# Second expert layer: TensorE's instructions in written order, the small work in pieces between a tile's control products

## The chip, the cores and the metric

The kernel runs on one core of one Trainium2 chip. The metric is the device time of the whole program in microseconds, as a median over runs: 3760.18 us of three runs, 3752.28 to 3766.32. Five engines work side by side and meet through semaphores: TensorE (PE, matrix products, with its weight loads as PEld), VectorE (DVE), ScalarE (ACT), GpSimd (POOL) and SyncE (SP, which issues transfers).

## The reference

The program is a network of four levels, each made of an attention over a context, a self-attention and a feed-forward layer. `x` is 16 x 64 x 256, so 1024 tokens of 256 numbers. The change is in the feed-forward layer of level 1, "the second expert layer" here:

```python
x = x + _L1_ffn_ref(_layernorm(x, axis=-1), ...)

def _inl(ctrl, xs, vs, mu):
    a, b, g = jnp.split(ctrl, 3, axis=-1)
    v_next = jax.nn.sigmoid(a) * vs - jax.nn.softplus(b) * (xs - mu)
    x_next = xs + DT * jax.nn.sigmoid(g) * v_next          # DT = 0.1
    return (x_next, v_next)

logits = _gelu(xf @ router_w1 + router_b1) @ router_w2 + router_b2
topk_p, topk_i = jax.lax.top_k(jax.nn.softmax(logits, axis=-1), K)   # K = 2 of E = 8
topk_p = topk_p / jnp.sum(topk_p, axis=-1, keepdims=True)
v = jnp.zeros_like(xf); integrated = xf
for _ in range(ITERS):                                      # ITERS = 2
    ctx = jnp.concatenate([integrated, v], axis=-1)
    shared_ctrl = _gelu(ctx @ shared_w1 + shared_b1) @ shared_w2 + shared_b2
    x_sh, v_sh = _inl(shared_ctrl, integrated, v, mu)
    ...
    ctrl = _experts(ctx_e, flat_idx, expert_w1, expert_b1, expert_w2, expert_b2)
    x_r, v_r = _inl(ctrl, x_e, v_e, mu)                     # both picks, weighted with topk_p
    x_next = sw * x_sh + (1.0 - sw) * x_r                   # v_next in the same way
    halt = jax.nn.sigmoid(_gelu(integrated @ halt_w1 + halt_b1) @ halt_w2 + halt_b2)
    integrated = integrated + halt * (x_next - integrated)
    v = v + halt * (v_next - v)
refined = _gelu(integrated @ refine_w1 + refine_b1) @ refine_w2 + refine_b2
out = xf + integration_weight * refined
```

Every token thus takes two rounds. In each it gets three controls of 3 x 256 numbers: one shared, and one from each of the two experts the router picked for it. Each expert's inner row has 64 numbers.

## The kernel before

`l1_ffn` (L1460) holds the layer. The 1024 tokens are two halves, `a` and `b`, of four tiles of 128 tokens each (`Half`, L1532). A half keeps on the chip its state `xi` and `v` and the sum `dx` (tokens on the partitions), and `cT`, the same `xi` and `v` turned, so that the 512 numbers of `ctx` lie on the partitions.

The steps of the layer are functions, called one after the other:

- `start(s)` normalises the half's four tiles into `xi`, turns them into `cT` (`self.transpose`, L152: four 128 x 128 transposes for two tiles at L160, then one copy out of PSUM on VectorE, L124, and one on ScalarE, L126) and has GpSimd add `xi` to the residual.
- `route(s)` makes the router: a product with Gelu (`gelu_t`: the product at L1549, the Gelu at L1550), the logits `pl` (L1570), softmax, ranks, a one-hot `hots` of each pick (L1578), turned into `hotT` (L1584, copied at L1586), and the two weights `wk`.
- `hidden(s, it)` makes the inner rows: `sT` of the shared expert and halt gate, four chunks `eT` of all eight experts (each chunk a product of 128 x 512 and its Gelu; two passes in round 0, four in round 1, in which `v` is no longer zero), then the halt product `ph` (L1606) and its sigmoid.
- `pick(s, i)` multiplies `eT` by the pick's one-hot: four products that spread the one-hot over the inner rows (L1614), each followed by a product on VectorE that writes `eh` (L1615).
- `control(s, it, i)` makes a control: `i` is -1 for the shared one, 0 and 1 for the picks. For each pair of tiles it fills one buffer `pc` of three banks. Each block of 256 columns starts with a product of the biases (L1632), followed by one product of the shared inner rows (L1636) or by four of `eh` (L1639). Round 0 has two blocks, round 1 three. Then ScalarE takes tanh of the gates (L1643, L1645) and the absolute value (L1646), and VectorE the positive part `rb` (L1647). After both pairs: exponent (L1649) and logarithm (L1650) on ScalarE, `vn` on GpSimd (L1651), and on VectorE `sp` (L1652), `vn` (L1653), in round 1 two more rows with `a`, `g` (L1658), and the sums into `dx` and `v` (L1661 for the shared control, L1664 for a pick, one row of 128 x 256 for each tile).
- `update(s, it)` moves `xi` by `dx` and the halt gate (L1671), turns it, and in round 0 does the same with `v` (L1676).
- `refine(s)` makes the output: four Gelu chunks `fT`, four output tiles `po` (L1686), each with three rows after it: `y` on VectorE, `y` on GpSimd, and the sum into the residual.

PSUM holds two buffers under the tag "mm", which the products of `gelu_t`, the turns, `pl`, `hotT`, `pick`, `ph` and `po` share in the order in which they are written, and two under "pc" for the controls. A product that starts a new buffer waits for the readers of the one before last.

The biases of the controls, `bias2`, are built ahead of the halves, in three steps of `part`, `raw` and `bias2` on VectorE (L1505 to L1507), and `expand`, the matrix of the picks, at L1514.

The order of the calls is this, from L1692 on:

```python
start(a); hidden(a, 0); route(a); start(b)
control(a, 0, -1); pick(a, 0); route(b); pick(a, 1); control(a, 0, 0); hidden(b, 0); control(a, 0, 1)
pick(b, 0); control(b, 0, -1); update(a, 0); pick(b, 1); control(b, 0, 0); hidden(a, 1); pick(a, 0)
control(b, 0, 1); control(a, 1, -1); pick(a, 1); update(b, 0); control(a, 1, 0); hidden(b, 1); pick(b, 0)
control(a, 1, 1); control(b, 1, -1); pick(b, 1); update(a, 1); control(b, 1, 0); control(b, 1, 1)
refine(a); update(b, 1); refine(b)
```

It is the order in which the instructions are recorded. A scheduler then orders each engine's instructions by its own plan, and may bring an instruction forward past others of its engine. An instruction handed to `keep_in_program_order` keeps its place among the others that were handed to it. The helpers `self.mm` and `self.tr` (L2450) do that for products and transposes while `self.pinned` is true; other stages use them, and this layer calls `nc.tensor.matmul` and `nc.tensor.transpose` itself, which leaves TensorE's order to the scheduler.

Of the kernel before, what the change touches and what calls it, by code (L numbers as in the profile page):

```python
# [64 lines left out]
class Sections:  # L65
# [1394 lines left out]
    def l1_ffn(self):  # L1460
# [3 lines left out]
        with ExitStack() as ctx:  # L1464
# [79 lines left out]
            def gelu_t(out, w, cT, bias, nk, lo=0):  # L1544

                m = out.shape[0]
                pm = ps.tile([m, N], F32, tag="mm", name="gelu_t")
                for c in range(nk):
                    nc.tensor.matmul(pm, w[:, c, lo : lo + m], cT[:, c, :], start=(c == 0), stop=(c == nk - 1))  # L1549
                nc.scalar.activation(out, pm, AF.Gelu, bias=bias)  # L1550

            def start(s):
                mv = sb2.tile([P, TT, 2], F32, tag="ln_mv", name="ln_mv")
                for t in range(TT):
                    st = sb2.tile([P, 6], F32, tag="ln_st", name="ln_st", bufs=3)
                    nc.vector.bn_stats(st, s.x[:, t, :])
                    nc.vector.bn_aggr(mv[:, t, :], st)
                r = self.rstd(sb2, mv[:, :, 1], 1e-5, "ln_r")
                for t in range(TT):
                    nc.vector.tensor_scalar(  # L1560
                        s.xi[:, t, :], s.x[:, t, :], mv[:, t, 0:1], r[:, t : t + 1], ALU.subtract, ALU.mult)
                self.transpose(ps, s.xi, s.cT[:, 0:2], tag="mm")
                nc.gpsimd.tensor_tensor(s.x, s.x, s.xi, ALU.add)

            def route(s):
                rT = sb2.tile([HID, N], F32, tag="rT", name="rT", bufs=1)
                gelu_t(rT, rw1, s.cT, self.v(k + "router_b1")[:HID], KC)
                pl = ps.tile([P, TT, E], F32, tag="mm", name="pl")
                for t in range(TT):
                    nc.tensor.matmul(pl[:, t, :], rT[:, t * P : (t + 1) * P], rw2, start=True, stop=True)  # L1570
                probs = sb2.tile([P, TT, E], F32, tag="probs", name="probs")
                nc.vector.tensor_tensor(probs, pl, rb2.unsqueeze(1).to_broadcast([P, TT, E]), ALU.add)
                self.softmax_small(sb2, probs, E)
                rank = self.ranks(sb2, probs, E)
                s.hotT = []
                for i in range(2):
                    hot = sb2.tile([P, TT, E], F32, tag="hot", name="hot")
                    nc.vector.tensor_scalar(hot, rank, float(i), None, ALU.is_equal)  # L1578
                    nc.vector.tensor_copy(
                        hots[i][:, :, : 3 * E].rearrange("p t (j e) -> p t j e", e=E),  # L1580
                        hot.unsqueeze(2).to_broadcast([P, TT, 3, E]))
                    pt = ps.tile([P, TT, P], BF16, tag="mm", name="hotT", padded_shape=[P, 2 * TT, P])
                    for t in range(TT):
                        nc.tensor.transpose(pt[:, t, :], hots[i][:, t, :], identb)  # L1584
                    hT = sb.tile([P, N], BF16, tag=f"hotT{i}{s.i}", name="hotT")
                    nc.vector.tensor_copy(hT, pt.rearrange("p t n -> p (t n)"))  # L1586
                    s.hotT.append(hT)
                    nc.vector.tensor_tensor(hot, hot, probs, ALU.mult)
                    nc.vector.tensor_reduce(s.wk[:, i, :], hot, AX.X, ALU.add)
                den = sb2.tile([P, TT], F32, tag="den", name="den")  # L1590
                nc.vector.tensor_tensor(den, s.wk[:, 0, :], s.wk[:, 1, :], ALU.add)
                nc.vector.reciprocal(den, den)
                nc.vector.tensor_scalar(den, den, swt[:, 1:2], None, ALU.mult)
                nc.vector.tensor_tensor(s.wk, s.wk, den.unsqueeze(1).to_broadcast([P, 2, TT]), ALU.mult)

            def hidden(s, it):

                nk = 4 if it else KC
                s.sT = sb2.tile([P, N], F32, tag="sT", name="sT")
                gelu_t(s.sT, shw1, s.cT, self.v(k + "sh_b1"), nk)  # L1600
                s.eT = sb.tile([P, 4, N], F32, tag=f"eT{s.i}", name="eT")
                for c in range(4):
                    gelu_t(s.eT[:, c, :], ew1, s.cT, self.v(k + "expert_b1")[:, c : c + 1], nk, c * P)
                ph = ps.tile([P, TT], F32, tag="mm", name="ph")
                for t in range(TT):
                    nc.tensor.matmul(ph[:, t : t + 1], s.sT[:, t * P : (t + 1) * P], hw2, start=True, stop=True)  # L1606
                sigmoid(s.halt, ph, hb)

            def pick(s, i):

                eh = sb2.tile([P, 4, N], F32, tag="eh", name="eh")
                for c in range(4):
                    pm = ps.tile([P, N], F32, tag="mm", name="pick")
                    nc.tensor.matmul(pm, expand[:, c * P : (c + 1) * P], s.hotT[i], start=True, stop=True)  # L1614
                    nc.vector.tensor_tensor(eh[:, c, :], s.eT[:, c, :], pm, ALU.mult)  # L1615
                s.eh = [*getattr(s, "eh", [None, None])]
                s.eh[i] = eh

            def control(s, it, i):
# [6 lines left out]
                for q in range(TT // 2):  # L1626
                    pc = ps.tile([P, 3, 2, D], F32, tag="pc", name="pc")
                    for j in range(2):
                        tok = slice((2 * q + j) * P, (2 * q + j + 1) * P)
                        for n, at in enumerate(blocks):  # L1630
                            cols = slice(at, at + D)
                            nc.tensor.matmul(  # L1632
                                pc[:, n, j, :], shared if i < 0 else s.hotT[i][:, tok], bias2[:, cols],
                                start=True, stop=False)
                            if i < 0:
                                nc.tensor.matmul(pc[:, n, j, :], s.sT[:, tok], sw2[:, cols], start=False, stop=True)  # L1636
                                continue
                            for c in range(4):
                                nc.tensor.matmul(  # L1639
                                    pc[:, n, j, :], s.eh[i][:, c, tok], ew2[:, c, cols], start=False, stop=(c == 3))  # L1640
                    two = slice(2 * q, 2 * q + 2)
# [5 lines left out]
                    nc.vector.tensor_scalar(rb[:, two], pc[:, 0], 0.0, None, ALU.max)  # L1647

# [10 lines left out]
                for acc, new in ((s.dx, g), (s.v, vn))[: 2 - it]:  # L1659
# [3 lines left out]
                    for t in range(TT):  # L1663
                        nc.vector.scalar_tensor_tensor(  # L1664
                            acc[:, t, :], new[:, t, :], s.wk[:, i, t : t + 1], acc[:, t, :], ALU.mult, ALU.add)

            def update(s, it):
                h = sb2.tile([P, TT], F32, tag="h", name="h")
# [4 lines left out]
                self.transpose(ps, s.xi, s.cT[:, 0:2], tag="mm")  # L1673
                if not it:
                    for t in range(TT):
                        nc.vector.tensor_scalar(s.v[:, t, :], s.v[:, t, :], s.halt[:, t : t + 1], None, ALU.mult)  # L1676
                    self.transpose(ps, s.v, s.cT[:, 2:4], tag="mm")

            def refine(s):
                fT = sb.tile([P, 4, N], F32, tag=f"eT{s.i}", name="fT")  # L1680
                for c in range(4):
                    gelu_t(fT[:, c, :], fw1, s.cT, self.v(k + "refine_b1")[:, c : c + 1], KC, c * P)
                for t in range(TT):
                    pm = ps.tile([P, D], F32, tag="mm", name="po", padded_shape=[P, 512])
                    for c in range(4):
                        nc.tensor.matmul(pm, fT[:, c, t * P : (t + 1) * P], fw2[:, c, :], start=(c == 0), stop=(c == 3))  # L1686
# [3 lines left out]
                    nc.vector.tensor_tensor(s.x[:, t, :], s.x[:, t, :], y, ALU.add)  # L1690

            a, b = Half(0), Half(1)  # L1692
            start(a)
            hidden(a, 0)
            route(a)
            start(b)
            control(a, 0, -1)
            pick(a, 0)
            route(b)
            pick(a, 1)  # L1700
            control(a, 0, 0)
            hidden(b, 0)
            control(a, 0, 1)
            pick(b, 0)
            control(b, 0, -1)
            update(a, 0)
            pick(b, 1)
            control(b, 0, 0)
            hidden(a, 1)
            pick(a, 0)  # L1710
            control(b, 0, 1)
            control(a, 1, -1)
            pick(a, 1)
            update(b, 0)
            control(a, 1, 0)
            hidden(b, 1)
            pick(b, 0)
            control(a, 1, 1)
            control(b, 1, -1)
            pick(b, 1)  # L1720
            update(a, 1)
            control(b, 1, 0)
            control(b, 1, 1)
            refine(a)
            update(b, 1)
            refine(b)
# [1094 lines left out]
```

## Time and profile before

| what | value |
| --- | --- |
| median of three runs | 3760.18 us (3752.28, 3760.18, 3766.32) |
| the profiled execution | 3753.96 us, of it 3752.2 span, granted TensorE clock 0.959 |
| the layer in it | first turn 2009.95 us, last product ends 2331.03 us |
| products and transposes in the layer | 1224 records, 289.92 us busy |
| VectorE, ScalarE, GpSimd busy in the layer | 175.09, 127.02, 36.29 us |

Times below are microseconds from the start of the span. The costliest lines of the layer by busy time (columns: line, engine, operation, output from inputs, shapes, count, then total us and mean ns of one, then idle time of that engine just before them and what ended it):

```profile
L1639 PE MATMUL pc<-ew,eh 128*128 128x256 f32 x640 | 158.8, 391 | 0.0
L1549 PE MATMUL gelu_t<-cT,ew 128*128 128x512 f32 x96 | 42.6, 594 | 0.1
L1651 POOL TENSOR_TENSOR vn<-xi,row_L_ffn_router_b 128x1024 f32<-128x1024 f32 x12 | 26.1, 2177 | 216.2 <-DVE g L1658 80.7 <-DVE v L1664 75.4 <-DVE v L1661 30.2
L1636 PE MATMUL pc<-sw,sT 128*128 128x256 f32 x80 | 23.5, 399 | 0.0
L1615 DVE TENSOR_TENSOR eh<-eT,pick 128x512 f32<-128x512 f32 x32 | 21.2, 682 | 7.7 <-PE pick L1614 7.3
L1650 ACT ACT_TABLE_LOAD x12 | 15.4, 1283 | 0.2
```

An f32 product is recorded in several passes, which is why L1639 has 640 records; "x1", "x8" in a timeline count records that follow each other without a gap. A mean of one is a mean over pipelined records, so sums of a line's busy time show its weight, and a wait shows in the timeline as a bracket behind the row: its length, the engine and the line that ended it. `ACT_TABLE_LOAD` stands where ScalarE changes to a function of another table.

### The profile page before, as it was taken

The numbers are of one execution on the slowest core, as the hardware profiler recorded it, in microseconds if no ns is written. First come the engines' busy times: TensorE is split into PE (matmuls) and PEld (weight loads), VectorE is DVE, ScalarE is ACT, GpSimd is POOL, SyncE is SP. The second block draws the span as 40 slices with busy tenths as digits, with TensorE's granted clock in tenths as the row PEclk, the third lists the DMA queues.
The fourth block names the chain that finished last, engine by engine and source line by source line (L and its number), as shares of the span: only waits on it lengthen the run. The fifth ranks groups of instructions, "written<-read, shape, count | busy, mean of one in ns | idle before, by whom it ended". The sixth has DMA issues, their size and how long they took to land.

```text
span 3752.2 us, 70803 instructions
## 1 busy us (share of the span) xinstructions
PE 3440.3 (92%) x30966; PEld 2187.8 (58%) x30966; DVE 1974.1 (53%) x3676; ACT 1451.3 (39%) x2076; POOL 1291.0 (34%) x787
## 2 busy tenths in 40 slices
PE   8999999996999969999977988999999789999986
PEld 4555555563665645555545666667767555555554
DVE  5344333436555546656657554577767665333346
ACT  2333333333444414444423443466666612111213
POOL 1555555562011123333321001577777630000012
PEclk9999999998999979999989999999999989999997
DMA  4111001101332344343101001111111004111640
GB/s 145 38 38 38 31 27 38 38 10 35 105 96 87 111 158 163 127 146 110 37 26 40 1 6 44 68 56 38 56 38 38 11 2 174 43 36 30 278 180 13
DMA packets 106123, 258.66 MB, mean 69 GB/s; under 512 B 9203, under 2 KB 74483, under 8 KB 103510
## 3 DMA queue, kind: packets, MB, share of 16 engines
q1 hardware_dynamic: 97366, 222.68, 16.6%
q10 hardware_dynamic: 6912, 27.27, 2.3%
q8 instruction: 243, 3.98, 0.4%
q0 software_dynamic: 1536, 4.20, 0.4%
q14 instruction: 66, 0.54, 0.0%
HBM read 248.34 MB, written 5.77 MB: 68 GB/s over the span
## 4 chain that ended last, share of the span: by engine, by line
PE 77%; DVE 12%; ACT 7%; issue 2%; DMA 1%; POOL 1%; SPq 0%; ACTq 0%; DVEq 0%; POOLq 0%
PE sc L2452 15%; PE pk L2452 15%; PE lin L2452 7%; PE acc L2452 6%; PE lin_t L2452 5%; ACT e L327 5%; PE pu L2452 4%; PE lin L194 3%; PE gate L2017 3%; PE up L2017 3%; PE pc L1639 3%; PE prz L2452 2%; PE gelu_t L1549 2%; PE turn L2457 2%; PE pa L2452 1%
## 5 line engine op out<-in xcount | busy, mean ns | idle before, releaser
L2385 POOL TENSOR_TENSOR tot<-tot,e 128x1024 f32<-128x1024 f32 (+1 forms) x340 | 802.9, 2361 | 374.5 <-ACT e L327 251.2
L270 DVE TENSOR_REDUCE m<-sc 128x4 f32<-128x2048 f32 x96 | 220.1, 2293 | 271.3 <-PE sc L2452 270.2
L1779 DVE SCALAR_TENSOR_TENSOR e<-sc,row_L_xattn_nbias,free 128x2048 f32<-128x2048 f32 x104 | 244.3, 2349 | 121.8 <-PE sc L2452 116.3
L1781 ACT ACTIVATE e<-e 128x2048 f32<-128x2048 f32 x104 | 198.7, 1910 | 243.2 <-DVE e L1779 243.2
L327 ACT ACTIVATE e<-sc 128x2048 f32<-128x2048 f32 x104 | 195.2, 1877 | 241.2 <-PE sc L2452 239.6
L2452 PE MATMUL sc<-qb,kT 32*128 32x128 f32 x6656 | 244.8, 283 | 36.6 <-DVE m L284 12.3
L2452 PEld LDWEIGHTS sc<-qb,kT 32*128 32x128 f32 x6656 | 205.9, 187 | 80.6 <-issue 24.5
L2452 PE MATMUL acc<-e,v 128*32 128x128 f32 x6656 | 226.6, 276 | 6.4 <-ACT e L1782 6.4
L2452 PEld LDWEIGHTS acc<-e,v 128*32 128x32 f32 x6656 | 170.3, 110 | 105.7 <-issue 95.1
L2452 PE MATMUL pk<-cT,wk 128*128 128x512 f32 (+1 forms) x512 | 207.0, 534 | 3.6 <-DVE rows L300 3.6
L2452 PE MATMUL pk<-wv,cT 128*128 128x256 f32 x832 | 209.8, 394 | 0.0
L1782 ACT ACTIVATE e<-e 128x2048 f32<-128x2048 f32 x104 | 198.7, 1911 | 3.3
L2452 PE MATMUL pk<-cT,wkv 128*128 128x512 f32 (+1 forms) x512 | 197.2, 526 | 0.0
L2452 PE MATMUL pk<-wkv,cT 128*128 128x256 f32 x832 | 196.3, 386 | 0.0
L2452 PEld LDWEIGHTS pk<-wv,cT 128*128 128x128 f32 x832 | 149.7, 190 | 75.5 <-issue 58.2
L2452 PEld LDWEIGHTS pk<-wkv,cT 128*128 128x128 f32 x832 | 153.3, 190 | 28.3 <-issue 4.3
L1639 PE MATMUL pc<-ew,eh 128*128 128x256 f32 x640 | 158.8, 391 | 0.0
L2452 PE MATMUL pu<-cn,e 128*64 128x257 f32 (+1 forms) x1248 | 146.5, 391 | 12.9 <-POOL e L1186 12.9
L2452 PE MATMUL sc<-kT,qb 32*128 32x512 f32 (+2 forms) x1536 | 140.8, 465 | 14.9 <-DVE m L270 2.3
L2021 ACT ACTIVATE g<-gate 128x512 f32<-128x512 f32 x68 | 40.6, 597 | 292.2 <-PE gate L2017 292.2
L1176 POOL TENSOR_TENSOR e<-e,mx 128x512 f32<-128x512 f32 x96 | 81.8, 883 | 194.7 <-DVE mx L1175 194.7
L2022 DVE TENSOR_TENSOR hT<-up,g 128x512 f32<-128x512 f32 x68 | 47.0, 692 | 178.8 <-PE up L2017 174.6
(519 smaller groups left out, 6339.5 us busy)
## 6 DMA issues: line engine op xcount, KB each, us to landing
cT<-in_ctx_t SPq DMA_DIRECT2D x128, 832.0 KB, 6.1
cn<-in_ctx_n SPq DMA_DIRECT2D x32, 1664.0 KB, 12.6
piece<-in_ctx_n ACTq DMA_DIRECT2D x32, 640.0 KB, 3.9
w<-in_L_attn_W SPq DMA_DIRECT2D x8, 1024.0 KB, 7.2
piece<-in_ctx_n ACTq DMA_DIRECT2D x16, 384.0 KB, 3.5
w<-in_L_ffn_W SPq DMA_DIRECT2D x16, 256.0 KB, 4.8
down<-in_L_ffn_w_down SPq DMA_DIRECT2D x16, 256.0 KB, 2.7
gate<-in_L_ffn_w_gate SPq DMA_DIRECT2D x16, 256.0 KB, 2.7
```

What stands on the lines that cost most here:

```text
L194: nc.tensor.matmul(pm, xT[:, k, t * P : (t + 1) * P], w[:, k, :], start=(k == 0), stop=(k == kc - 1))
L270: nc.vector.tensor_reduce(x.m4[:, g, :, i], pm, AX.X, ALU.max)
L327: nc.scalar.activation(e, pm, AF.Exp, scale=0.25)
L1176: pin(nc.gpsimd.tensor_tensor(p.e, p.e, p.mx.unsqueeze(2).to_broadcast(p.shape), ALU.subtract))
L1549: nc.tensor.matmul(pm, w[:, c, lo : lo + m], cT[:, c, :], start=(c == 0), stop=(c == nk - 1))
L1639: nc.tensor.matmul(pc[:, n, j, :], s.eh[i][:, c, tok], ew2[:, c, cols], start=False, stop=(c == 3))
L1779: nc.vector.scalar_tensor_tensor(e16, pm16, nb, free[:, at : at + P].unsqueeze(1).to_broadcast([P, 16, P]), ALU.add, ALU.mult)
L1781: nc.scalar.activation(e, e, AF.Relu)
L1782: nc.scalar.activation(e, e, AF.Square)
L2017: nc.tensor.matmul(pm[-1], w[:, k, n * P : (n + 1) * P], xT[:, k, tok], start=(k == 0), stop=(k == KC - 1))
L2385: nc.gpsimd.tensor_tensor(tot[:w], x.first if c == 1 else tot[:w], e[:w], ALU.add)
L2452: ins = self.nc.tensor.matmul(*args, **kw)
```

## The change

TensorE's instructions in the layer are handed to `keep_in_program_order`: `gelu_t`, `route`, `hidden`, `pick`, `control` and `refine` call `self.mm` and `self.tr`, and `self.pinned` is true from the first half's start to the layer's end. So that small work can be written between the products of a control, the steps become generators, each of which stops (`yield`) after a piece: `turn` after a pair of tiles, `route` after its Gelu, its ranks, its turned one-hots with the weights, `hidden` after each Gelu chunk and after the halt gate, `pick` after each chunk, `control` after each tile of the first pair, after the first pair's evacuations, after the third tile, and at its end; `update` after each turned pair, `refine` after each chunk and each output tile. `go` takes a number of pieces from such a generator, `between` takes one piece of a control and then the named pieces of others, and so on, and then the rest of the control.

`turn` stands in place of `self.transpose` in this layer; it does the same transposes and copies. `start` only normalises now, two tiles at a time, each pair with a reciprocal root of its own, so that there are two more square roots, reciprocals and scalings for the two halves. The list of calls is replaced. Its sequence of controls is the same as before.

```diff
                 for c in range(nk):
-                    nc.tensor.matmul(pm, w[:, c, lo : lo + m], cT[:, c, :], start=(c == 0), stop=(c == nk - 1))
+                    self.mm(pm, w[:, c, lo : lo + m], cT[:, c, :], start=(c == 0), stop=(c == nk - 1))
...
+            def turn(src, dst):
+                for t in range(0, TT, 2):
+                    pt = ps.tile([P, KC, 2, P], F32, tag="mm", name="tr")
+                    for c in range(KC):
+                        for j in range(2):
+                            self.tr(pt[:, c, j, :], src[:, t + j, c * P : (c + 1) * P], self.ident)
+                    for c in range(KC):
+                        self.copy(dst[:, c, t * P : (t + 2) * P], pt[:, c].rearrange("p j x -> p (j x)"))
+                    yield
...
             def start(s):
...
+                for p in range(TT // 2):
...
+                    r = self.rstd(sb2, mv[:, :, 1], 1e-5, "ln_r")
...
-                self.transpose(ps, s.xi, s.cT[:, 0:2], tag="mm")
-                nc.gpsimd.tensor_tensor(s.x, s.x, s.xi, ALU.add)
...
             def control(s, it, i):
...
+                        if j == 0:
+                            yield
...
                     nc.vector.tensor_scalar(rb[:, two], pc[:, 0], 0.0, None, ALU.max)
+                    if q == 0:
+                        yield
...
             def update(s, it):
...
-                self.transpose(ps, s.xi, s.cT[:, 0:2], tag="mm")
                 if not it:
                     for t in range(TT):
                         nc.vector.tensor_scalar(s.v[:, t, :], s.v[:, t, :], s.halt[:, t : t + 1], None, ALU.mult)
-                    self.transpose(ps, s.v, s.cT[:, 2:4], tag="mm")
+                yield from turn(s.xi, s.cT[:, 0:2])
+                if not it:
+                    yield from turn(s.v, s.cT[:, 2:4])
...
+            def go(it, n=99):
+                for _ in range(n):
+                    if next(it, self) is self:
+                        break
+
+            def between(ct, *others):
+                for i, some in enumerate(others):
+                    go(ct, 1)
+                    for it, n in some:
+                        go(it, n)
+                go(ct)
...
             a, b = Half(0), Half(1)
+            self.pinned = True
             start(a)
...
+            go(turn(a.xi, a.cT[:, 0:2]))
+            nc.gpsimd.tensor_tensor(a.x, a.x, a.xi, ALU.add)
             start(b)
...
+            ra, ha = route(a), hidden(a, 0)
+            go(ra, 1)
+            go(ha, 1)
+            go(ra, 1)
+            go(ha, 2)
+            go(turn(b.xi, b.cT[:, 0:2]))
+            nc.gpsimd.tensor_tensor(b.x, b.x, b.xi, ALU.add)
+            rb, hd = route(b), hidden(b, 0)
+            go(rb, 1)
+            go(ha)
+            go(hd, 1)
+            go(ra)
+            go(rb, 1)
+            p0, p1 = pick(a, 0), pick(a, 1)
+            between(control(a, 0, -1), [(p0, 1)], [(p0, 1)], [(p0, 1)], [(p0, 1)])
+            between(control(a, 0, 0), [(p1, 2)], [(p1, 2)], [(rb, 9)], [(hd, 2)])
+            p0 = pick(b, 0)
+            go(hd)
+            between(control(a, 0, 1), [(p0, 1)], [(p0, 1)], [(p0, 1)], [(p0, 1)])
+            p1 = pick(b, 1)
+            between(control(b, 0, -1), [(p1, 1)], [(p1, 1)], [(p1, 1)], [(p1, 1)])
+            ua, ha = update(a, 0), hidden(a, 1)
+            between(control(b, 0, 0), [], [(ua, 2)], [(ua, 2)], [(ha, 2)])
+            p0 = pick(a, 0)
+            between(control(b, 0, 1), [(ha, 2)], [(ha, 9), (p0, 1)], [(p0, 1)], [(p0, 2)])
+            p1 = pick(a, 1)
+            between(control(a, 1, -1), [(p1, 1)], [(p1, 1)], [(p1, 1)], [(p1, 1)])
+            ub, hd = update(b, 0), hidden(b, 1)
+            between(control(a, 1, 0), [(ub, 2)], [(ub, 2)], [(hd, 2)], [(hd, 2)])
+            p0 = pick(b, 0)
+            between(control(a, 1, 1), [(hd, 9), (p0, 1)], [(p0, 1)], [(p0, 1)], [(p0, 1)])
+            p1 = pick(b, 1)
+            between(control(b, 1, -1), [(p1, 1)], [(p1, 1)], [(p1, 1)], [(p1, 1)])
+            ua, fa = update(a, 1), refine(a)
+            between(control(b, 1, 0), [], [(ua, 1)], [(ua, 1)], [(fa, 1)])
+            between(control(b, 1, 1), [(fa, 1)], [(fa, 1)], [], [])
+            go(fa)
+            go(update(b, 1))
+            go(refine(b))
+            self.pinned = False
```

In the names of the prediction, a piece of a control is one tile's products; the four entries of a `between` stand after the first, second, third and fourth entry of its `yield`s. `control` yields after tile 0, after tile 1 with the first pair's evacuations, after tile 2, and at its end, after the rows of VectorE.

## The prediction

> **What bounds the kernel now.** I read the engine shares first, then the second expert layer by stretches, then what TensorE waited for inside it, and last the order of time around those waits. The layer runs from its first turn at 2009.95 us to its last product, which ends at 2331.03: 321 us, 8.6% of the span.
>
> ```profile
> PE 3440.3 (92%) x30966; PEld 2187.8 (58%) x30966; DVE 1974.1 (53%) x3676; ACT 1451.3 (39%) x2076; POOL 1291.0 (34%) x787
> ```
>
> TensorE (PE) is busy almost throughout. In the layer it is idle in some stretches and in others not at all (columns: stretch, its length, then busy time and instruction count of each engine):
>
> ```profile
> 2049.70:2096.40 46.70, 46.56 (x213) 33.14 (x212) 21.80 (x50) 20.22 (x27) 2.48 (x2) 1.00 0.00 1
> 2096.40:2121.00 24.60, 20.33 (x96) 15.64 (x96) 22.96 (x35) 11.70 (x17) 5.35 (x2) 0.93 0.00 1
> 2160.60:2191.60 31.00, 26.94 (x129) 21.47 (x128) 24.35 (x36) 11.58 (x17) 4.17 (x2) 0.94 0.00 1
> 2009.90:2332.70 322.80, 289.92 (x1224) 202.90 (x1224) 175.09 (x293) 127.02 (x170) 36.29 (x22) 0.95 0.02 5
> ```
>
> So 32.9 us without a matmul is all that an order of TensorE can win by filling gaps. The waits by line, 2005 to 2335 us (total, times, longest):
>
> ```profile
> PE pc L1632 <- DVE rb L1647: 7.2, 3, 3.0
> PE pick L1614 <- DVE eh L1615: 5.7, 5, 1.8
> PE tr L160 <- DVE xi L1671: 4.0, 3, 1.4
> ```
>
> A control's first product waits for `rb` to empty its buffer, a pick for the pick two before, a turn for the inner rows. In order of time such a wait costs more than its length, and a short one almost nothing more:
>
> ```profile
> 2099.34 0.27 PE L1632 MATMUL pc<-bias,hotT 128*128 128x256 bf16 x1 [2.98 <-DVE rb L1647]
> 2099.45 3.38 PE L1639 MATMUL pc<-ew,eh 128*128 128x256 f32 x8
> 2104.81 1.89 PE L1639 MATMUL pc<-ew,eh 128*128 128x256 f32 x8
> 2114.80 0.94 PE L160 MATMUL tr<-cst,xi 128*128 128x128 f32 x4 [1.24 <-DVE xi L1671]
> 2115.58 0.60 PE L1639 MATMUL pc<-ew,eh 128*128 128x256 f32 x2
> ```
>
> After 2.98 us of idling the first eight expert passes took 3.38 instead of 1.89. After 2.38 us (2304.16) the same is seen, 3.50 for four `gelu_t` passes against 1.98 at 2299.80. After 1.24 to 1.4 us it is 0.1 to 0.3. I call this 1.6 us "the slow start" and charge it to every wait of 2.4 us or more.
>
> VectorE (DVE) is what sets these waits, and three of its rows matter:
>
> ```profile
> 2106.39 2.22 DVE L1671 SCALAR_TENSOR_TENSOR xi<-dx,h,xi 128x256 f32<-128x256 f32 x1
> 2109.67 0.47 DVE L1671 SCALAR_TENSOR_TENSOR xi<-dx,h,xi 128x256 f32<-128x256 f32 x1
> 2163.50 0.69 DVE L1647 TENSOR_SCALAR rb<-pc 128x512 f32<-128x512 f32 x1
> 2164.10 1.22 DVE L1658 SCALAR_TENSOR_TENSOR g<-g,vn 128x1024 f32<-128x1024 f32 x1
> 2165.63 1.67 DVE L1664 SCALAR_TENSOR_TENSOR dx<-g,wk,dx 128x256 f32<-128x256 f32 x4
> ```
>
> One `xi` row takes 2.22 instead of 0.47 because it runs inside GpSimd's `vn` (2105.42 to 2108.33). And `rb` at 2163.50 stands ahead of `g` and of the eight `dx` and `v` rows of the control before, so TensorE gets its buffer early.
>
> **The change, part by part.** It adds no product and no transpose (16449 matmuls in both builds). The normalising goes by pairs of tiles: two more square roots, reciprocals and scalings, at 0.2 us or less each. Six more table loads of 1.28 us come on ScalarE. SP and the transfers are unmoved, and outside this layer all engines keep their order. What moves is the order, and not only TensorE's: the new recording order also moves VectorE's and ScalarE's. So I walked the layer through the order of the changed build, instruction by instruction, with the semaphore each one waits for and durations from the rows of before: expert block 1.84 us, shared block 0.54, pick 0.22, gelu of two or four chunks 1.72 or 3.43, halt product 0.81, pair turned 0.43, output tile 1.73; VectorE's 1024-wide rows 1.13 to 1.14 from start to start, `eh` and `rb` 0.60 to 0.69, one `dx` or `v` 0.40; ScalarE 0.49 for a 512-wide row followed by another, exponent and logarithm 1.06, table 1.28, Gelu 0.69. "a00" is half a, iteration 0, pick 0; "a0s" its shared control. Each term is waits plus slow starts, after minus before.
>
> *Opening: -0.4.* Before: 2.60+0.77+2.07+1.11+0.66+1.19+0.95+0.28+0.77 = 10.4 of waits and 4.1 of slow matmuls (3.35 for 1.72 at 2014.62, three shared blocks at 1.06 for 0.54, 0.9 at 2046.29). After: half b is turned early, but its two copies out of PSUM stand on VectorE behind the ranks and the whole building of the bias (three times 0.47+0.87+0.93 from start to start, 0.33 for `expand`, some 2.4 for the ranks and one-hots: 9.5 us after the router's softmax, which ends 2.0 after the router's product). TensorE has 4.8 us of inner rows and turns to cover it; the copies cost 1.4 more, so the router of b waits 8.0. With 3.6 of small waits and two slow starts, less 0.75 for a first turn that starts earlier, 14.1.
>
> *Inner rows of b: +6.1.* Before, the scheduler laid a00's products between them and nothing waited. Now four gelus follow each other with two buffers. ScalarE first owes tanh and abs (1.2), exponent 1.06 and a table 1.28 before the first Gelu 0.69, 4.3 us after a00's last product; two gelus cover 3.4: 0.9. Then table, logarithm, table, Gelu, another 4.3, against one gelu of 1.7: 2.6, and a slow start.
>
> *Shared control b0s: 0.* From the last product before it, the logarithm ends 6.3 us later (2091.1 to 2097.4), then `sp` 1.14 and `rb` 0.6, 8.1 in all; four pieces of 1.09 and four picks cover 5.2. The picks do not wait any more, `rb` does, as before: 2.9 for 2.98.
>
> *Update of a: +6.7.* The turns of `xi` are now pinned after tile pair 0 of b00, 9.0 us after `rb` freed the buffer. VectorE then needs `vn` 1.14, `rb` 0.6, `g` 1.13, eight accumulations 3.2, `sp` 1.14, `xi` 2.2, `vn` 1.13, `xi` 0.4: 11.0, wait 2.0. The second pair is 5.2 behind (`g`, `v`, `dx`, `rb`, two `xi` beside GpSimd, 2.6), wait 4.7, slow start 1.6. Before it was 1.24 and 0.34, because expert products stood between the turns.
>
> *Shared control a1s: +4.2.* In the new order `rb` of its first pair comes after `g` and the eight accumulations of b01. Logarithm's end at 6.5, `sp`, `vn`, `eh`, `g`, 3.2, `rb` make 14.4; four pieces of 1.63 and picks cover 7.4: 7.0 and a slow start, against 1.30+1.36+1.75.
>
> *Update of b: +4.4.* Same construction: 7.1 us of products against 7.5 of VectorE (0.4), then `g`, `xi`, `dx` beside GpSimd 2.4, `xi`, less one turn: 3.9, slow start 1.6; before 1.40 and 0.1.
>
> *Shared control b1s and a's second update: -2.0.* Logarithm 7.0, then `sp`, `eh`, two `vn`, `g`, `rb` 5.8, cover 7.4: 5.4 and 1.6; the turns no longer wait. Before: 1.79+1.35+2.89+1.38 and 1.7.
>
> *End: +5.3.* The fourth Gelu of a's refinement waits behind tanh, abs, table, exponent and table, 5.9 after the last control; the fourth gelu and three of four passes cover 2.9: 3.1. Then b's last update (logarithm 2.3, 4.7 of `sp` to `g`, 1.6, 1.7, with a's eight output rows between) comes 5.0 after a's last output product, 0.6 for the copies, two slow starts: 11.9, against 6.6 before (1.32+2.38+0.16+1.01, 1.7).
>
> Sum: -0.4+6.1+0+6.7+4.2+4.4-2.0+5.3 = +24.3 us. The next stage starts from the layer's last sums (its `ln_st` rows follow at 2332.65), so nothing hides it. On the profiled execution's 3753.96 this gives 3778; that execution lies 6.2 below the median of the three, 3760.18, so I forecast 3784.
>
> The Trainium skill, page "TensorE: Matmul & The Clock Gate", section "HAM oscillation", warns of TensorE gaps over about 3.4 us, after which the clock halves for such a window; it speaks against holding TensorE to one order. By its threshold only six of my nine long waits would pay (1.7 each), and four of the trace's own slow starts should not exist; the sum would be about 2 us higher. The rows at 2099.45 and 2304.16 decide for 2.4.
>
> Bounds: the slow start is 0.1 (row after 1.4 us) to 1.75 (2164.24), doubtful at inner rows and end, -3.2 together. Whether an `xi` or `a` row meets GpSimd is 0 or 1.75 in four places, two of them drawn as met and doubtful: -3.5 to +3.5. The opening's bias rows could run 0.07 slower each when not overlapped, or a `part` row take 2.21 (2019.38): -4 to +3. Gaps that order alone leaves between short pieces: 0 to +5. So +12 to +36 for this case, 3772 to 3796.
>
> **The rivals.** *Faster, by gaps filled.* The picks and turns do stand between products, and if `rb` were there when TensorE arrives, the four places at 2099, 2164, 2180 and 2241 and the turn at 2114.80 would cost nothing: 4.5+4.4+1.5+9.1+1.6 = 21 less, 3739. It decides at the shared controls: the chain to `rb` must be no longer than the cover, 5.2 or 7.4 us. For it: picks wait 5.7 now. Against: the chains above are 8.1, 14.4 and 12.8, and a pinned engine can't go round them. Chance 0.11.
>
> *No measurable change.* If ScalarE's order costs nothing at the inner rows and half at the end (the gelus overlap what I count in line), 24-6-3 = +15, 3775; with half the two updates as well +9, 3769. For it: 32.9 us of idleness remain about the same. Against: the waits are in the built order. Chance 0.27.
>
> *Worse still.* Nine slow starts, each `xi` beside GpSimd and short gaps at every insertion: +36, 3796; inside the 0.62 of slower.
>
> That the change doesn't do what it says is excluded: the built order is the written one.
>
> **Numbers.** A measurement of this kernel tells about 0.5%, 18.8 us, from no change. Slower beyond that 0.62, within 0.27, faster 0.11; the forecast case's own range is 3772 to 3796, the range with the middle case 3760 to 3800.
>
> **What would show it.** In the changed profile: a TensorE wait near 8 us at b's router product for `cT`; two waits before turns for `xi`, together near 11 us; a wait near 7 us for `rb` ahead of a10; waits for picks near nothing; a wait of 3 us at the first output product. If the turns' waits are under 2 us and `rb` waits stay at 7 us in sum, the forecast is wrong and the faster case holds. If the opening's wait is missing, VectorE's copies went ahead of the bias and the sum falls by 8.

## The result, and the profile after

The changed kernel takes 3783.47 us (median of five runs, 3783.32 to 3785.01) against 3754.79 (five runs, 3752.28 to 3766.32) for the kernel before. The ratio is 1.0065, with a 95% interval of 1.0051 to 1.0079. It is slower, and the forecast of 3784 holds, though part of that agreement is luck, as the end of the next section but one shows.

I measure the layer as the stretch from the start of the attention's last output product (2003.45 before, 2006.31 after) to the next stage's first turn (2335.99 and 2362.22). The view by stretches gives for it, first before, then after (stretch, length, busy time and count of PE, PEld, DVE, ACT, POOL, granted TensorE clock, then transfers):

```profile
2003.45:2335.99 332.54, 291.02 (x1228) 203.55 (x1228) 183.46 (x333) 127.84 (x174) 38.35 (x26) 0.95 0.04 11
```

```profile
2006.31:2362.22 355.91, 297.94 (x1227) 208.70 (x1228) 180.89 (x337) 135.83 (x182) 39.57 (x26) 0.91 0.03 11
```

The layer costs 23.4 us more. Idle time of TensorE grows from 332.54 - 291.02 = 41.5 to 58.0, so 16.5 of the 23.4 are waits; 6.9 are the same products taking longer, at a granted clock of 0.91 instead of 0.95 (the slow starts of the prediction).

The waits by line of the changed kernel, 2005 to 2365 us (total, times, longest):

```profile
PE tr L2514 <- DVE xi L1700: 17.3, 6, 6.9
PE pc L2509 <- DVE rb L1672: 14.4, 3, 6.2
PE gelu_t L2509 <- DVE hot L1606: 6.6, 1, 6.6
...
PE gelu_t L2509 <- ACT eT L1550: 3.2, 2, 2.4
PE po L2509 <- ACT fT L1550: 3.0, 1, 3.0
```

Picks, which waited 5.7 us before, have left the list. Turns wait 17.3 instead of 4.0, and `rb` holds a control's first product for 14.4 instead of 7.2. In order of time (start, duration, what, and in brackets the wait ahead of it):

```profile
2035.14 3.65 PE L2509 MATMUL gelu_t<-cT,rw 128*64 128x512 f32 x4 [6.58 <-DVE hot L1606]
...
2078.85 3.54 PE L2509 MATMUL gelu_t<-cT,ew 128*128 128x512 f32 x4 [2.38 <-ACT eT L1550]
...
2106.81 0.27 PE L2509 MATMUL pc<-bias,hotT 128*128 128x256 bf16 x1 [2.83 <-DVE rb L1672]
2106.91 1.89 PE L2509 MATMUL pc<-ew,eh 128*128 128x256 f32 x8
...
2116.13 0.33 PE L2514 MATMUL tr<-cst,xi 128*128 128x128 f32 x1 [1.81 <-DVE xi L1700]
2117.66 0.55 PE L2514 MATMUL tr<-cst,xi 128*128 128x128 f32 x3 [1.20 <-DVE xi L1700]
2122.26 1.29 PE L2514 MATMUL tr<-cst,xi 128*128 128x128 f32 x4 [4.05 <-DVE xi L1700]
...
2180.50 0.39 PE L2509 MATMUL pc<-bias,hotT 128*128 128x256 bf16 x1 [6.20 <-DVE rb L1672]
...
2266.84 0.40 PE L2509 MATMUL pc<-bias,hotT 128*128 128x256 bf16 x1 [5.40 <-DVE rb L1672]
...
2324.61 7.43 PE L2509 MATMUL po<-fw,fT 128*128 128x256 f32 x26 [3.02 <-ACT fT L1550]
...
2338.91 2.15 PE L2514 MATMUL tr<-cst,xi 128*128 128x128 f32 x8 [6.87 <-DVE xi L1700]
```

The 6.20 at 2180.50 is read from VectorE's order of time around it:

```profile
2175.45 1.22 DVE L1685 SCALAR_TENSOR_TENSOR g<-g,vn 128x1024 f32<-128x1024 f32 x1
2176.59 0.48 DVE L1691 SCALAR_TENSOR_TENSOR v<-vn,wk,v 128x256 f32<-128x256 f32 x1
2176.99 1.67 DVE L1691 SCALAR_TENSOR_TENSOR dx<-g,wk,dx 128x256 f32<-128x256 f32 x4
2178.57 1.27 DVE L1691 SCALAR_TENSOR_TENSOR v<-vn,wk,v 128x256 f32<-128x256 f32 x3
2179.76 1.28 DVE L1672 TENSOR_SCALAR rb<-pc 128x512 f32<-128x512 f32 x2
```

`rb`, which frees the buffer, stands behind `g` and the eight sums of the control before. In the kernel before it stood ahead of them (2163.50).

The 6.58 at 2035.14, b's router, is read there too. The profile puts it down to `hot`, but the copies out of the turned tiles (`cT`) had ended just before, and they came right behind the last step of the biases:

```profile
2033.21 1.00 DVE L1507 SCALAR_TENSOR_TENSOR bias<-part,cst,bias 32x768 bf16<-32x768 bf16 x1
...
2034.26 0.74 DVE L124 COPY cT<-tr 128x256 f32<-128x256 f32 x2
```

### The profile page after: what moved, and what is told of

Its sections match the earlier page's. It is cut to its first block, busy times and chain, and to the rows that moved or that the text cites. A ratio compares the mean times of both kernels' runs of the same rounds, so it can differ in the third digit from the quotient of the medians.

```text
span 3781.5 us, 70787 instructions
## 1 busy us (share of the span) xinstructions
PE 3447.2 (91%) x30952; PEld 2189.7 (58%) x30966; DVE 1970.6 (52%) x3680; ACT 1459.0 (39%) x2084; POOL 1292.7 (34%) x787
## 3 DMA queue, kind: packets, MB, share of 16 engines
q1 hardware_dynamic: 97366, 222.68, 16.5%
## 4 chain that ended last, share of the span: by engine, by line
PE 77%; DVE 13%; ACT 7%; issue 2%; DMA 1%; POOL 1%; SPq 0%; ACTq 0%; DVEq 0%; POOLq 0%
PE sc L2509 15%; PE pk L2509 15%; PE lin L2509 7%; PE acc L2509 6%; PE lin_t L2509 5%; ACT e L327 4%; PE pu L2509 4%; PE pc L2509 4%; PE lin L194 3%; PE gate L2074 3%; PE up L2074 3%; PE prz L2509 2%; PE gelu_t L2509 2%; PE turn L2514 2%; PE pa L2509 1%
## 5 line engine op out<-in xcount | busy, mean ns | idle before, releaser
L2509 PE MATMUL sc<-cT,qT 128*64 128x512 f32 (+1 forms) x768 | 141.3, 520 | 2.4 <-ACT scs L1156 1.9
```

The lines of the kernel that those rows point to most:

```text
L2509: ins = self.nc.tensor.matmul(*args, **kw)
```

## The experiments

Every time named "stretch" is the one just defined: 332.5 before, 355.9 after. (The first expectations give 333.9 for the kernel before; its next stage starts at 2335.99, which makes it 332.5.) Each stretch is read from one profiled execution. A slow start can come or go from one kernel to the next where the same wait stands, as the last section shows, so a difference of 2 to 3 us between two stretches says little by itself. In the text b0s, a1s and b1s are the shared controls of b in round 0 and of a and b in round 1, as in the prediction.

**The order kept, TensorE not held to it.**

```diff
-            self.pinned = True
+            self.pinned = False
             start(a)
```

> The changed kernel with its written order and its pieces, but TensorE not held to them. The stretch from the attention's last output product to the next stage's first turn is 333.9 us before and 355.9 after the change. Theory (the time is lost where TensorE is held at a turn or an inner row although other products are ready): the waits at the two updates (7.1 and 3.3 us), at b's inner rows (3.2) and part of the one at the opening (6.6) shrink, with their slow starts; the waits for rb at the shared controls stay, because VectorE's order stays. Stretch 338 to 344. Rival (the new recording order on VectorE and ScalarE costs, not the holding): stretch 350 or more.

Stretch 338.6; 3762.96 us against 3756.05, ratio 1.0010 (0.9998 to 1.0021). The waits of this kernel:

```profile
PE pc L2509 <- DVE rb L1672: 14.4, 3, 6.2
PE tr L2514 <- DVE xi L1700: 9.1, 3, 6.7
PE pc L2509 <- DVE bias L1507: 5.7, 1, 5.7
```

The `rb` waits are unchanged to the tenth, inner rows wait for nothing, and of the turns' 17.3 us 9.1 are left, 6.65 of them at the end, where nothing is ready to go ahead. At the opening little is gained: the router's 6.58 turns into 5.70 at a's first control, which waits for its biases. For the rest the theory holds: holding costs 17.3 us of stretch. What else the change moves, the recording order of the other engines above all, costs the other 6.1.

**The old calls, undivided, with TensorE held.** In the kernel before, every `nc.tensor.matmul` and transpose of the layer becomes `self.mm` and `self.tr`, with `self.pinned` true around the calls.

> The kernel before, its calls in their old order and undivided, with TensorE held to the written order. Theory: holding is what costs and the pieces repay a part of it. Four picks in a row then wait for each other's eh (0.69 against 0.22, about 1.4 us for each of eight groups), and the turns of an update stand right behind a shared control with nothing before them (some 7 us more for a and for b). Stretch 375 to 400, that is 20 to 45 us over the changed kernel. Rival (the pieces themselves cost, by short gaps at every insertion): stretch under 356.

Stretch 399.1; 3829.05 us, ratio 1.0179 (1.0155 to 1.0202). Turns wait up to 10.8 us, one pick 10.6. So the theory holds and the rival falls: holding costs the undivided calls 66.6 us, and the pieces with this list win back 43.2 of that.

**Turns one to three pieces later.**

```diff
-            between(control(b, 0, 0), [], [(ua, 2)], [(ua, 2)], [(ha, 2)])
+            between(control(b, 0, 0), [], [], [], [(ua, 2)])
-            between(control(b, 0, 1), [(ha, 2)], [(ha, 9), (p0, 1)], [(p0, 1)], [(p0, 2)])
+            between(control(b, 0, 1), [(ua, 2), (ha, 2)], [(ha, 2)], [(ha, 9), (p0, 2)], [(p0, 2)])
-            between(control(a, 1, 0), [(ub, 2)], [(ub, 2)], [(hd, 2)], [(hd, 2)])
+            between(control(a, 1, 0), [], [(ub, 2)], [(ub, 2), (hd, 1)], [(hd, 2)])
```

> The changed kernel with the turns of the first updates written later: a's after the whole of b's control 0 and after the first tile of control 1, b's after tile 1 and tile 2 of a's control 0; a's inner rows move back by as much. Theory (a turn is early for its inner rows of VectorE by a fixed time): waits at the turns fall from 10.4 us to 2 or less, their slow starts go too, and nothing else grows; stretch 343 to 348. Rival (VectorE as a whole sets the pace here, so the wait comes back at the next place that needs it, the shared control of a): the wait for rb there grows by most of what the turns save, stretch 352 or more.

Stretch 345.4; 3766.14 us, ratio 1.0027 (1.0014 to 1.0040). In both updates no turn waits any more. Two inner rows wait for the copies instead (2.27 and 0.48), and the shared control of a still waits 6.20. The theory holds but for these 2.75 us at the inner rows, which it had not allowed for; the rival's wait at the shared control did not grow. (What this expectation calls the inner rows of a turn, and the prediction at its first waits too, are the `xi` rows on VectorE, not the inner rows of `hidden`.)

**The shared controls' positive part on ScalarE.**

```diff
+                    if i < 0:
+                        nc.scalar.activation(rb[:, two], pc[:, 0], AF.Relu)
+                    else:
-                    nc.vector.tensor_scalar(rb[:, two], pc[:, 0], 0.0, None, ALU.max)
+                        nc.vector.tensor_scalar(rb[:, two], pc[:, 0], 0.0, None, ALU.max)
```

> The changed kernel with the positive part of the three shared controls made by ScalarE (Relu, behind abs) and not by VectorE, so that the buffer comes free without VectorE's queue. Theory (rb is late because it stands behind sp, vn, g and eight sums of the control before on VectorE): the waits of 2.83, 6.20 and 5.40 us become what ScalarE's chain leaves, logarithm 7 us after the last product and then tanh, tanh, abs and relu, 2.2, against a cover of 5.2 or 7.4: 1.0 to 2.5 each, and slow starts go; stretch 344 to 349. Rival (ScalarE's exponent and logarithm are what is late, VectorE only comes last): the waits shrink by no more than 1 us each, stretch 353 or more.

Stretch 351.4; 3779.50 us, ratio 1.0056 (1.0036 to 1.0075): between the two. At b0s the wait falls from 2.83 to 1.94, as the theory had it. TensorE in order of time:

```profile
2166.77 0.27 PE L2512 MATMUL pc<-bias,hotT 128*128 128x256 bf16 x1 [1.47 <-ACT rb L1673]
...
2177.10 0.48 PE L2517 MATMUL tr<-cst,xi 128*128 128x128 f32 x1 [4.65 <-DVE xi L1703]
2178.63 0.90 PE L2517 MATMUL tr<-cst,xi 128*128 128x128 f32 x3 [1.05 <-DVE xi L1703]
2180.16 0.47 PE L2517 MATMUL tr<-cst,xi 128*128 128x128 f32 x1 [0.63 <-DVE xi L1703]
2182.97 0.90 PE L2517 MATMUL tr<-cst,xi 128*128 128x128 f32 x3 [2.33 <-DVE xi L1703]
...
2256.22 0.37 PE L2512 MATMUL pc<-bias,hotT 128*128 128x256 bf16 x1 [5.15 <-ACT rb L1673]
```

At a1s, a's second shared control, it holds too: 1.47 instead of 6.20. But b's turns, which follow behind the first two tiles, now wait 8.7 us (4.65+1.05+0.63+2.33) instead of 3.3. At b1s the wait stays at 5.15, for a cause I had not named, read on ScalarE:

```profile
2254.60 0.60 ACT L1670 ACTIVATE a<-pc 128x512 f32<-128x512 f32 x1 [2.38 <-DVE vn L1686]
```

The tile `a` has one buffer, so its next tanh waits until VectorE's second `vn` has read the old one. A second buffer for `a` wasn't tried.

**Both at once**, later turns and ScalarE's positive part:

> Later turns and the shared controls' positive part on ScalarE in one kernel. Alone, the later turns left 345.4 us and 6.20 of wait at a's second shared control; ScalarE alone left 351.4, with 1.47 there but 8.7 instead of 3.3 at b's turns. Theory (what ScalarE's part saves at that control came back at the turns behind it, because the rows of VectorE that make xi take as long as before): with turns one tile of 5.5 us later, they wait about 3 us and not 8.7, and the control 1.5; stretch 337 to 343. Rival (the turns waited there for another reason, such as ScalarE's longer queue): they still wait 5 us or more, stretch 345 or more.

Stretch 345.4, the same as later turns alone to a hundredth; 3772.78 us against 3757.33, ratio 1.0029 (1.0015 to 1.0044). The shared control waits 1.47, and b's turns 4.0 (0.56+0.98+2.48) where they had waited for nothing. I had allowed for 3 us of it, and for 2.4 to 8.4 of gain; there was none. The turns are nearer to the theory's 3 than to the rival's 5, the stretch is the rival's. Of the 4.73 us saved at the control 4.02 came back at the turns; with the small changes elsewhere TensorE waits 1.6 us less in all (48.9 against 50.5), and slow starts take these 1.6 back (296.5 us busy against 294.9), so that the equal stretch is in part chance. So a wait in front of a control is little loss by itself: while TensorE waits there, VectorE works off the rows that the turns need next. Moving one row of 0.7 us to ScalarE leaves the others as long as they were.

**Biases after b's turning.** The three `part`, `raw`, `bias2` steps are recorded after `go(turn(b.xi, ...))`.

> The changed kernel with the three steps that build the controls' biases recorded after the turning of half b, so that VectorE copies b's turned tiles out first. The stretch from the attention's last output product to the next stage's first turn is 355.9 us after the change (and 332.5 before it). Theory (the wait of 6.58 us at b's router is VectorE working off the biases): it falls to 1 to 3 us and one slow start goes, the first control still finds its biases; stretch 348 to 352. Rival (the biases are needed as soon as the copies are, so the wait moves to the first control's first product): a wait of 3 us or more there, stretch 354 or more.

Stretch 346.7; 3772.73 us against 3760.40, ratio 1.0033 (1.0017 to 1.0048). In order of time:

```profile
2032.24 1.90 PE L2509 MATMUL gelu_t<-cT,rw 128*64 128x512 f32 x4 [0.88 <-DVE hots L1589]
...
2073.04 1.98 PE L2509 MATMUL gelu_t<-cT,ew 128*128 128x512 f32 x4 [2.38 <-ACT eT L1546]
...
2099.45 0.37 PE L2509 MATMUL pc<-bias,hotT 128*128 128x256 bf16 x1 [2.83 <-DVE rb L1668]
2099.61 3.27 PE L2509 MATMUL pc<-ew,eh 128*128 128x256 f32 x8
```

The wait falls from 6.58 to 0.88, and the router's passes from 3.65 to 1.90. That is 7.5 of the 9.2 gained, a little more than the theory's 348 to 352 allowed. Another 1.6 is the slow start at the inner rows, which is gone (1.98 instead of 3.54). A new one at b0s (3.27 instead of 1.89) costs nothing: a's first turn behind it waits 0.36 instead of 1.81. The last section takes up why they moved.

**Inner rows as cover.** If each wait is a chain longer than what is written to cover it, a better order follows: inner rows, which need nothing of VectorE once the turned tiles are copied out, go behind the other half's last expert control, ahead of the shared control. The biases stay late, and a's remaining inner rows go ahead of b's router product (`go(ha)` before `go(rb, 1)`). The core of the new list:

```diff
-            between(control(b, 0, 0), [], [(ua, 2)], [(ua, 2)], [(ha, 2)])
+            between(control(b, 0, 0), [(p1, 1)], [(p1, 1)], [(p1, 1)], [(p1, 1), (ua, 2)])
-            between(control(b, 0, 1), [(ha, 2)], [(ha, 9), (p0, 1)], [(p0, 1)], [(p0, 2)])
+            between(control(b, 0, 1), [(ua, 2)], [], [(ha, 2)], [(ha, 3)])
-            between(control(a, 1, -1), [(p1, 1)], [(p1, 1)], [(p1, 1)], [(p1, 1)])
+            between(control(a, 1, -1), [(ha, 9), (p0, 1)], [(p0, 1)], [(p0, 1)], [(p0, 1)])
-            between(control(a, 1, 0), [(ub, 2)], [(ub, 2)], [(hd, 2)], [(hd, 2)])
+            between(control(a, 1, 0), [(p1, 1)], [(p1, 1)], [(p1, 1), (ub, 2)], [(p1, 1), (ub, 2)])
-            between(control(a, 1, 1), [(hd, 9), (p0, 1)], [(p0, 1)], [(p0, 1)], [(p0, 1)])
+            between(control(a, 1, 1), [], [(hd, 1)], [(hd, 1)], [(hd, 3)])
...
```

The other controls follow the same pattern: `[], [(hd, 1)], [(hd, 1)], [(hd, 2)]` in a's control 1 of round 0, the second pick's pieces in the control 0 of the same half, a's last turns in the third and fourth place of b's control 0 in round 1, and two of a's refining chunks in b's control 1.

> The changed kernel with the biases after b's turning, and with another written order, still held: the inner rows of the next half stand behind the last expert control of the other and in its last tiles, ahead of the shared control; picks stand in the two controls that follow; turns of an update stand in the last tiles of the other half's control 0. Theory (each wait of the changed kernel is a chain of VectorE and ScalarE longer than the products written to cover it, and inner rows, which need no VectorE, are the cover): waits for rb at a's and b's second shared control fall from 6.2 and 5.4 to 2 or less, turns wait 2 or less, the end stays at some 10; stretch 318 to 332, no slower than the kernel before. Rival (the total of VectorE and ScalarE between two updates sets the pace, so that the waits only move): waits of 15 us or more in all outside opening and end, stretch 340 or more.

Stretch 312.2, 20.4 below the kernel before; 3739.76 us against 3760.40, ratio 0.9949 (0.9933 to 0.9965). It beats both. Against the changed kernel 29.7 us of waits are gone, and the same products take 14.0 us less (283.9 us busy), at a granted clock of 0.97 instead of 0.91. The stretch lies 5.8 below the forecast range: the end waits 7.5 and not some 10, and the expectation names no slow starts. The largest of its waits inside the layer:

```profile
PE tr L2510 <- DVE xi L1569: 4.4, 1, 4.4
PE po L2505 <- ACT fT L1546: 4.0, 2, 2.6
PE pick L2505 <- ACT eT L1546: 3.3, 1, 3.3
```

No control waits for `rb`, and the turns of the updates wait 0.4 at most. What is left lies at the opening, at b's first shared control and at the end.

**The same order, not held.**

> The same written order as in the run with the inner rows as cover, but TensorE not held to it. Theory (holding costs only where a wait is left): within 6 us of the held one, stretch 316 to 332. Rival (the scheduler's own plan is better than any written order): 8 us or more below the held one.

Stretch 312.0; 3740.02 us, ratio 0.9949 (0.9928 to 0.9970): no difference to the held one, as the theory had it, and like that one below the range. Where the order leaves little to wait for, the scheduler's freedom is worth nothing that shows here.

**One chunk earlier at b's first shared control.** In that kernel, `control(a, 0, 1)` gets `[(hd, 1)]` four times, and b's halt product goes behind `control(b, 0, -1)`.

> The order with the inner rows as cover (312.2 us), with b's four chunks one after each tile of a's control 1 in round 0 instead of two of them behind it, and b's halt product behind its shared control. Theory (the 1.0, 3.3 and 1.5 us at b's first shared control are picks and the halt product held up by two Gelus between exponent and logarithm on ScalarE): those waits fall to 2 or less in sum, and rb, which loses 1.7 us of cover, waits 2 or less; stretch 306 to 311. Rival (the cover lost is worth as much as the picks gain): rb waits 3 us or more, stretch 311 or more.

Stretch 311.0; 3739.07 us against 3757.33, ratio 0.9942 (0.9922 to 0.9962). The 5.8 us at picks and halt product are gone, as the theory had it, but `rb` now waits 3.40 for the cover that was taken: the rival's price. The stretch stands where both ranges meet, and the gain of 1.2 us can't be told from nothing in the time.

## Why the prediction was right, and where not

The waits of TensorE at each place, in us (forecast and measured are those of the changed kernel; the opening's are without the first turn's 4.35, against 5.39 before):

| place | before | forecast | measured |
| --- | --- | --- | --- |
| opening | 10.4 | 11.6 | 9.8 |
| inner rows of b | 0 | 3.5 | 3.2 |
| shared control b0s | 3.0 | 2.9 | 2.8 |
| update of a | 1.2 | 6.7 | 7.1 |
| shared control a1s | 2.7 | 7.0 | 6.2 |
| update of b | 1.4 | 4.3 | 3.3 |
| b1s and a's second update | 7.4 | 5.4 | 5.4 |
| end | 4.9 | 8.7 | 10.5 |

All eight lie within 2 us of the forecast, and each has the cause that it named, the end only in part. The mechanism, chains of VectorE and ScalarE longer than the products written over them and an engine that can't go round, is shown by the runs that take it away: TensorE not held (-17.3), later turns (-10.5), late biases (-9.2), inner rows as cover (-43.7, together with late biases).

What was off:

- *End.* The wait at b's last turns is 6.87 and not 5.0. I let a's output rows lie between b's rows, at their own length only. But VectorE keeps its order: `sp` could start when the logarithm ended, at 2326.93, and stands behind the `y` of the second output tile, which itself waits for its product.

```profile
2328.62 0.42 DVE L1720 TENSOR_TENSOR y<-po,row_L_ffn_router_b 128x256 f32<-128x256 f32 x1 [1.16 <-PE po L2509]
2328.97 1.21 DVE L1679 TENSOR_TENSOR sp<-sp,rb 128x1024 f32<-128x1024 f32 x1
```

- *Opening.* The copies waited for the biases as forecast, 6.58 and not 8.0.
- *Inner rows.* The term stands in the sum as 6.1, but its parts, 0.9, 2.6 and 1.6, make 5.1; measured, 0.83+2.38 and 3.54-1.98 = 1.56, are 4.8. With the slip mended the sum is 23.3.
- *Slow start.* I charged 1.6 us to every wait of 2.4 and more. At b0s, after 2.83 us, the eight passes took 1.89 and paid nothing (2106.91). Elsewhere it was more than 1.6: at b's turns the half clock lasts 6.83 us (2191.25 to 2198.08) and costs some 2.9, half of the 5.9 us for which TensorE is busy in it.

The errors nearly cancel: +24.3 was forecast for the layer (23.3 with the slip mended), +23.4 measured. That is luck in part, for the two kinds are off in opposite ways: the prediction's terms hold some 18.4 us of waits and 4.7 of slow starts, the profile 16.5 and 6.9. The total agrees for a further reason, which I had not reckoned with. The profiled executions differ by 29.3 us in span, so 5.9 arise outside the layer, 2.9 ahead of it and 3.1 behind, where both kernels run the same instructions in the same order; and the median of the kernel before came out 5.4 lower with five runs than with three. With only one of the two, the forecast would have been 5 to 6 us off.

The rival "gaps filled" fell because `rb` isn't there when TensorE arrives, as its own condition said; the order with the inner rows as cover shows that it holds as soon as the cover is long enough.

## What to carry to other kernels

Before an order is fixed by hand, write down for each wait point the chain that must end there, on every engine's own queue, and the products that cover it; in this layer a fixed order whose covers were a few microseconds too short lost 17.3 us against a scheduler that may go round. Cover is best made of work that doesn't need the engine that is late: here the inner rows ahead of the shared control; the order built on them is 20.4 us shorter than the kernel before. And a wait that is taken away in front of a late chain, while the chain stays as long, can come back at the next place that needs it (4.0 of 4.7 us here), so sum the rows of the chain, not the waits.

## What the runs showed of the hardware

The same wait doesn't always cost a slow start. At the inner rows, 2.38 us of waiting were followed by 3.54 us for four passes in the changed kernel (2078.85) and by 1.98 with late biases (2073.04). At b0s, 2.83 us were followed by 1.89 for eight passes (2106.91) and by 3.27 (2099.61). In the trace's record of the granted clock, the stretches at half clock inside these two executions last 3.41, 6.83, 10.24 us and more, always a multiple of 3.413 but for the last, which the end of the program cuts off. Their starts lie on one grid of 3.413 us from the first to the last, to 5 ns. That fits the Trainium skill, page "TensorE: Matmul & The Clock Gate", section "What's actually happening", which says that a free-running window of 3413 ns decides.

The traces also show what decides. Here are steps of that grid around the two waits of the changed kernel (step, length, TensorE's busy time and records, granted clock, then transfers):

```profile
2075.20:2078.61 3.41, 1.26 (x3) 1.00 0.00 0
2078.61:2082.02 3.41, 3.17 (x4) 0.50 0.01 2
2102.50:2105.92 3.42, 1.48 (x8) 1.00 0.00 0
2105.92:2109.33 3.41, 2.52 (x13) 1.00 0.00 0
```

At the inner rows one step holds 2.15 us without a product, and the next runs at half clock. The longer wait at b0s falls on two steps, 1.94 and 0.89, and costs nothing: the granted clock of the step behind them is 1.00. With late biases it is the other way round, 1.43 and 1.36 at the inner rows, and at b0s most of the wait in one step:

```profile
2095.57:2098.99 3.42, 1.04 (x6) 1.00 0.00 0
2098.99:2102.40 3.41, 2.95 (x8) 0.50 0.00 0
```

In the eleven stretches of this study a step at full clock with 2.0 us or more of idleness was followed by one at half clock in 78 of 78 cases, a step with less in 5 of 858. A step at half clock was followed by another in 80 of 80 cases where it held 0.7 us of idleness or more, and in 2 of 77 where it held less. A wait thus pays by how much of it falls into one step, and not by its length alone; neither the prediction's 2.4 us nor the 3.4 us of idleness that it sets against them is the limit here.

The same shows in stages that the change doesn't touch. The linear attention of level 2, before and after:

```profile
3043.88:3105.59 61.71, 49.87 (x853) 37.99 (x853) 47.15 (x92) 7.96 (x10) 14.72 (x5) 0.90 0.04 13
```

```profile
3067.43:3133.70 66.27, 54.47 (x852) 41.48 (x853) 47.24 (x92) 7.96 (x10) 14.71 (x5) 0.82 0.04 12
```

The same work takes 4.6 us more, all of it in TensorE's busy time, at a granted clock of 0.82 instead of 0.90. Other stages gain and lose too, so that 3.1 us are left behind the layer as a whole (1416.2 and 1419.3 us from the next stage's first turn to the end). That the shift by the layer moved these waits against the grid is the likely cause; it wasn't tried by itself. The 2.9 us ahead of the layer can't come from that shift: the last output product of the attention starts anywhere from 2001.2 to 2008.6 us in the eleven executions, whatever was changed behind it. Span less stretch lies between 3418.0 and 3428.0 us, with no tie to the change made.
